# One of four heads' exponentials turned by VectorE and DMA instead of TensorE

## The chip, the core and the metric

The kernel runs on one core of a Trainium2 chip. A core has TensorE (PE in the profile; PEld is its weight load), VectorE (DVE), ScalarE (ACT), GpSimd (POOL) and SyncE (SP), which here does nothing but issue DMAs, and 16 DMA engines that move data between DRAM and the on-chip memory. The engines run their own queues in order and wait for each other through semaphores. The metric is the device time of one execution in microseconds (us), as the median of several runs.

## What is computed

A layer over 16 sequences of 128 positions with 512 channels, each with a context of 2048 rows. It has three parts: cross-attention with 16 heads of 32 channels, a selective state-space block (Mamba) with an MLP, and a mixture-of-experts output. The change touches the first part alone:

```python
q = queries @ wq.T + bq
k = context @ wk.T + bk
v = context @ wv.T + bv
...
attn = jnp.einsum('bhnd,bhsd->bhns', q, k) * scale
attn = jax.nn.softmax(attn, axis=-1)
out = jnp.einsum('bhns,bhsd->bhnd', attn, v)
```

Everything is float32.

## The kernel before

**Steps.** The attention is cut into 256 steps `u` (`NU`): 16 sequences, for each four blocks of 512 context rows (`sb`), for each four groups of four heads (`hg`). One step handles 128 queries x 512 context rows for four heads. The rest of the layer rides along in the same loop: the keys and values of the next block of context (`product`, L240, in a scheme that saves products), the input projections, the scans and the output projections of the state-space block (from step 54 on the scans run beside the attention), so that each step carries the attention of four heads and a piece of other work. After step 255 the MLP and the experts follow (`feed`).

**The order is written by hand.** The pool is under a manual schedule: each engine runs its instructions in the order in which the Python code emits them. The loop at the end of `perceiver_layer` emits, in each step: the loads of the step on SyncE (`load_bc`, `load_ctx`, the entries of `loads`); `scores(u)`; `weighted(u - 1)`; `maxima(u)`; the first products of the next context block (`x_products`); `exps(u)`; the first scan; `hold` and `x_sums`, which empty the two product banks; the four `turn(u, i)`, with other pieces of PE work (`late`) before the last one where a bank is needed; the second scan; `inner` work on VectorE; and `y_products`, the second part of the products.

**What a step of attention does.** `scores` (L302) fills four PSUM banks, one per head: 128 queries on partitions, 512 context rows along. `maxima` (L310) takes each row's maximum with VectorE. `exps` (L320) writes the exponentials of the four heads into one tile `pr` (128 queries x 4 heads x 512 rows; one buffer) with ScalarE and keeps the row sums. The weighted product needs the context rows on partitions, so `turn(u, i)` transposes, for the i-th 128 rows, the 128x128 blocks of the four heads with TensorE against an identity (L333) into a PSUM bank. ScalarE copies that bank to the tile `pT` (L338); in most steps VectorE makes the copy for `i == 2` (L336). `weighted(u)`, emitted in the next step behind that step's scores, multiplies the values `v` by the four `pT` tiles (L346), the four heads on four groups of 32 output partitions:

```python
for i in range(4):
    for j in range(4):
        nc.tensor.matmul(avp[j * HD : (j + 1) * HD, hg, :], vts[...][...],
                         pts[u, i][:, j, :], start=(i == 0), stop=(i == 3))
```

**SyncE's queue.** All loads of the loop and the few stores go through SyncE, in program order. An issue waits there until the buffer that it fills is free, and what is behind it waits too. The `c` tiles of the context (L154), the weight tiles `ws` (six buffers, shared by the attention's weights L167 and L169, `win` L504 and `wout` L509) and the broadcast rows `bc` (L601, two buffers each) are loaded a step or more before they are used. The rows `bcd` are the one thing that goes through DRAM and comes back at once: written at L593, read at L601.

Of the kernel before, what the change touches and what calls it, by code (L numbers as in the profile page):

```python
# [8 lines left out]
FP = mybir.dt.float32  # L9
# [6 lines left out]
P = 128  # L16
# [18 lines left out]
def perceiver_layer(ctx: ExitStack, tc: tile.TileContext, a: dict, out: bass.AP):  # L35
    nc = tc.nc

    const = ctx.enter_context(tc.tile_pool(name="const", bufs=1))
    dram = ctx.enter_context(tc.tile_pool(name="dram", bufs=1, space=DRAM))

    ident = const.tile([P, P], FP, tag="ident", name="ident")
# [14 lines left out]
    zd = [dram.tile([NQ, D], FP, tag=f"zd{b}", name=f"zd{b}") for b in range(B)]  # L56
    xnd = [dram.tile([NQ, D], FP, tag=f"xnd{b}", name=f"xnd{b}") for b in range(B)]
    bcd = [dram.tile([2 * DS, GT], FP, tag=f"bcd{g}", name=f"bcd{g}") for g in range(B // GB)]

    mv = const.tile([P, B, 2], FP, tag="mv", name="mv")  # L60
    rstd = const.tile([P, B], FP, tag="rstd", name="rstd")
# [47 lines left out]
    with ExitStack() as es:  # L109
# [5 lines left out]
        pool = att.enter_context(tc.tile_pool(name="att", bufs=2))  # L115
# [9 lines left out]
        banks = [psum.tile([P, 512], FP, tag=f"s{j}", name=f"bank{j}") for j in range(4)]  # L125
        avp = psum.tile([P, 4, P], FP, tag="av", name="avp")
        hst = psum.tile([P, NH // 2, GT], FP, tag="h0", name="hst")
        pa = psum.tile([P, 2, 256], FP, tag="pa", name="pa")
        pc = psum.tile([P, 2, 256], FP, tag="pc", name="pc")
# [5 lines left out]
        scale = float(HD) ** -0.5  # L135
        nc.vector.tensor_scalar_mul(bq, bq, scale)

        ctx_t, kts, vts, qts, prs, pts, avs, stats, xts = ({} for _ in range(9))
        wfac, cfac, held = {}, {}, {}

        def heads(ps):
            return ps.rearrange("p (k q) -> p k q", q=P)

        def halves(ps):
            return ps.rearrange("p (k q) -> p k q", q=256)
# [36 lines left out]
        def split(u):  # L182
            return u // 16, u // 4 % 4, u % 4
# [113 lines left out]
        def scores(u):  # L297

            b, sb, hg = split(u)
            for j in range(4):  # L300
                rows = slice(j * HD, (j + 1) * HD)
                nc.tensor.matmul(  # L302
                    banks[j], qts[b][rows, hg, :], kts[u // 4, hg][rows, :], start=True, stop=True
                )
            del kts[u // 4, hg]
# [8 lines left out]
        def exps(u):  # L314
            b, sb, hg = split(u)
            nm, sm = stats[b]
            pr = pool.tile([P, 4, 512], FP, tag="pr", name=f"pr{u}", bufs=1)
            for j in range(4):
                h = hg * 4 + j
                nc.scalar.activation(  # L320
                    pr[:, j, :],
                    banks[j],
                    AF.Exp,
                    bias=nm[j][:, sb, hg : hg + 1],
                    accum_out=sm[:, sb, h : h + 1],
                )
            prs[u] = pr

        def turn(u, i, bank):

            ps = heads(banks[bank])
            for j in range(4):
                nc.tensor.transpose(ps[:, j, :], prs[u][:, j, i * P : (i + 1) * P], ident)  # L333
            pT = pool.tile([P, 4, P], FP, tag="pT", name="pT", bufs=4)
            if i == 2 and u % 16 > 2:
                nc.vector.tensor_copy(pT, ps)  # L336
            else:
                nc.scalar.copy(pT, ps)  # L338
            pts[u, i] = pT

        def weighted(u):

            b, sb, hg = split(u)
            for i in range(4):
                for j in range(4):
                    nc.tensor.matmul(  # L346
                        avp[j * HD : (j + 1) * HD, hg, :],
                        vts[u // 4, hg // 2, i // 2][
                            :, i % 2, hg % 2 * P + j * HD : hg % 2 * P + (j + 1) * HD
                        ],  # L350
                        pts[u, i][:, j, :],
                        start=(i == 0),
                        stop=(i == 3),
                    )
            for i in range(4):
                del pts[u, i]
            del prs[u]
            if hg == 3:
                t = keep.tile([P, 4, P], FP, tag="avs", name=f"avs{b}_{sb}", bufs=4)
                nc.scalar.copy(t, avp)  # L360
                avs[b, sb] = t
# [825 lines left out]
        for g in range(NG):  # L1187
            p = 32 * (g + 1)
# [36 lines left out]
        put(inner, NU, lambda: give_back(flat(pa)))  # L1225


        ways = (("k", pa, pc, "u2"), ("v", halves(banks[0]), halves(banks[1]), "u2v"))

        def first_products(of, ph):  # L1230
            x_products(of, 0, ph, *dict((w[0], w[1:3]) for w in ways)[of])
# [44 lines left out]
        ps = banks[2]  # L1276
# [8 lines left out]
        for u in range(last):  # L1285
            live = u < NU
            g, r = divmod(u - 32 - LAG, 32)
            scans = 0 <= g < NG

            made, phase = divmod(u + 3, 4)  # L1290
            makes = 0 < made < B * SB
            of, phase = ("k", "v")[phase // 2], phase % 2
            load_bc(u + 2 - 32 - LAG, 0)
            if u % 4 == 1 and made + 1 < B * SB:
                load_ctx(made + 1, ("c00", "c10", "c11"))
            if u % 4 == 2 and made + 1 < B * SB:
                load_ctx(made + 1, ("c01",))
            for f in loads.get(u, ()):
                f()
            if scans and u <= NU:  # L1300
                decays(g, r, 0)
            if u > NU:
                while fed < feeds * (u - NU) // (last - 1 - NU):
                    feed(fed)
                    fed += 1
                if scans:
                    decays(g, r, 0)
            load_bc(u + 1 - 32 - LAG, DS)
            if u == NU + 1:
                load_rows()  # L1310
            if live:
                scores(u)
            if 1 <= u <= NU:
                weighted(u - 1)
            if u == NU:
                att.close()
                give_back(*banks, flat(avp))
                open_ffn()
            for f in early.get(u, ()):
                f()  # L1320
            if u == NU + 8:
                load_wex()
            for f in head.get(u, ()):
                f()
            if live:
                maxima(u)
            if makes:
                x_products(of, made, phase, pa, pc)
            if live:
                exps(u)  # L1330

            turns = ("t1", "t2", "t3", "t4") if u % 16 == 5 else ("t1", "t2")
            if makes and u % 4 == 1:
                ctx_sums(made, turns)
            for f in between.get(u, ()):
                f()
            if 0 <= u + 1 - 32 - LAG < 32 * NG:
                inputs(*divmod(u + 1 - 32 - LAG, 32))
            if makes and u % 4 == 1 and len(turns) == 2:
                ctx_sums(made, ("t3", "t4"))  # L1340
            silu_third()
            if scans:
                scan(g, r, 0)
            if makes:
                hold(of, made, pa, "u1")
            if scans:
                decays(g, r, 1)
            if makes:
                x_sums(of, made, phase, pa, pc)

            after_turns = late.get(u, ())
            places = [banks[(3 + i) % 4] for i in range(len(after_turns))]
            if live and after_turns:
                if u % 4 == 0:
                    places = [flat(avp), *places[:-1]]
                elif u % 2 and makes and u not in behind:
                    places[-1] = flat(pc)

            ahead = live and u % 16 in (3, 10) and len(after_turns) == 1
            if ahead:
                after_turns[0](banks[3])
                after_turns, places = (), ()
            taken = sum(any(p is b for b in banks) for p in places)
            if live:
                for i in range(3 if taken else 4):
                    turn(u, i, i)
            if scans:
                scan(g, r, 1)  # L1370
            for f in middle.get(u, ()):
                f()
            for f, ps in zip(after_turns, places):
                if live:
                    f(ps)
                else:
                    ps = bank()
                    f(ps)
                    give_back(ps)
            if live and taken:  # L1380
                turn(u, 3, (3 + taken) % 4)
            for f in behind.get(u, ()):
                ps = flat(pc) if makes else banks[2] if live else bank()
                f(ps)
                if not live:
                    give_back(ps)
            for f in after.get(u, ()):
                f()
            for f in inner.get(u, ()):
                f()  # L1390
            if makes:
                y_products(of, made, phase, pa, pc)
                y_sums(of, made, phase, pa, pc)
            silu_second()
# [76 lines left out]
```

## Time and profile before

| | |
|---|---|
| runs | 3761.74 us median of 3 (3761.29 to 3770.05) |
| span of the profiled execution | 3760.5 us |
| TensorE busy | 3722.9 us, 99% |
| VectorE busy | 2706.2 us, 72% |
| ScalarE busy | 2446.9 us, 65% |
| GpSimd busy | 2112.4 us, 56% |
| granted TensorE clock | 0.998 |
| transposes of the exponentials, L333 | 4096 instructions, 508.2 us |
| copies of them by ScalarE, L338 | 816, 434.4 us |
| copies of them by VectorE, L336 | 208, 143.9 us |
| weighted products, L346 | 8192 instructions, 276.7 us |
| DMA | 548.42 MB, mean 146 GB/s |

The profile is one execution, taken by the hardware profiler. An engine's busy time is the time in which at least one of its instructions ran. A group of instructions is given by its source line, engine and operation, `out<-in` by the program's tile names, the count, the busy time of the group, the mean ns of one and the idle time of the engine just before them with what ended it. A view called the timeline lists instructions in order of time, with their start, their duration and their count where neighbours are merged; the chain that ended last follows back from the last instruction through whatever released each step. SyncE's rows are DMA issues; "to landing" counts from the issue until the data are there.

### The profile page before, as it was taken

How to read it: one execution, taken by the hardware profiler on the slowest of the kernel's cores; microseconds unless marked ns; L12 is line 12 of the kernel's file. 1: busy time of each engine (PE TensorE's matmuls, PEld its weight loads, DVE VectorE, ACT ScalarE, POOL GpSimd, SP SyncE). 2: the span in 40 equal slices, each digit the busy share in tenths (PEclk: the TensorE clock that was granted, in tenths of full speed). 3: DMA queues.
4: the chain of work that ended last, by engine and by line, in shares of the span. 5: the costliest groups of instructions: out<-in, count | busy, mean ns of one | idle time of the engine just before them, and what ended most of it. 6: DMA issues, size and time to landing. Idle time of an engine off the chain costs nothing.

```text
span 3760.5 us, 70389 instructions
## 1 busy us (share of the span) xinstructions
PE 3722.9 (99%) x26120; PEld 2851.7 (76%) x26120; DVE 2706.2 (72%) x4854; ACT 2446.9 (65%) x5848; POOL 2112.4 (56%) x1969
## 2 busy tenths in 40 slices
PE   9999999999999999999999999999999999999999
PEld 7878787778777887888787878787778776655655
DVE  3444445887878777877788778877887877778843
ACT  4555556777767776777677767776777775545431
POOL 2111213676767666765666666766675667567820
PEclk9999999999999999999999999999999999999999
DMA  3111122344444535353534453445444448676752
GB/s 102 35 40 43 49 71 83 127 152 150 132 165 142 158 115 186 124 165 116 190 124 149 136 184 128 150 135 172 141 151 139 162 166 312 205 267 244 248 191 82
DMA packets 343225, 548.42 MB, mean 146 GB/s; under 512 B 24368, under 2 KB 227408, under 8 KB 342624
## 3 DMA queue, kind: packets, MB, share of 16 engines
q1 hardware_dynamic: 342432, 543.27, 43.5%
q8 instruction: 206, 3.38, 0.4%
q14 instruction: 139, 1.14, 0.1%
q0 software_dynamic: 448, 0.63, 0.1%
HBM read 527.29 MB, written 16.52 MB: 145 GB/s over the span
## 4 chain that ended last, share of the span: by engine, by line
PE 94%; DVE 2%; DMA 1%; ACT 1%; issue 1%; POOL 0%; SPq 0%; DVEq 0%; ACTq 0%; POOLq 0%
PE pa L240 24%; PE pc L240 17%; PE bank L333 12%; PE bank L302 7%; PE avp L346 7%; PE bank L531 5%; PE bank L942 4%; PE bank L911 2%; PE bank L1043 2%; PE bank L472 2%; PE avp L399 1%; PE bank L716 1%; PE pc L716 1%; PE avp L942 1%; PE pa L911 1%; PE pc L531 1%
## 5 line engine op out<-in xcount | busy, mean ns | idle before, releaser
L310 DVE TENSOR_REDUCE nm<-bank 128x1 f32<-128x512 f32 x1024 | 635.5, 683 | 225.2 <-PE bank L302 225.0
L703 POOL TENSOR_TENSOR ysum<-ysum,w 128x512 f32<-128x512 f32 x384 | 500.2, 1303 | 487.4 <-DVE hst L666 309.0
L320 ACT ACTIVATE pr<-bank,nm 128x512 f32<-128x512 f32 x1024 | 690.6, 688 | 90.9 <-DVE nm L310 85.3
L652 POOL TENSOR_TENSOR w<-dx,bc 128x512 f32<-128x512 f32 x512 | 655.9, 1302 | 8.9
L687 DVE TENSOR_TENSOR_SCAN hst<-hst,w 128x512 f32<-128x512 f32 x459 | 561.1, 1222 | 42.8 <-ACT hst L673 33.6
L338 ACT COPY pT<-bank 128x512 f32<-128x512 f32 x816 | 434.4, 586 | 177.2 <-PE bank L333 173.2
L673 ACT ACTIVATE hst<-dt,alog 128x254 f32<-128x254 f32 x918 | 439.4, 479 | 112.0 <-DVE hst L666 95.8
L333 PE MATMUL bank<-ident,pr 128*128 128x128 f32 x4096 | 508.2, 273 | 3.3 <-ACT pr L320 2.8
L333 PEld LDWEIGHTS bank<-ident,pr 128*128 128x128 f32 x4096 | 468.2, 141 | 47.1 <-issue 11.1
L346 PEld LDWEIGHTS avp<-pT,v 128*32 128x32 f32 x8192 | 208.0, 109 | 194.4 <-issue 176.6
L690 DVE TENSOR_TENSOR w<-hst,bc 128x512 f32<-128x512 f32 x459 | 317.4, 692 | 20.8 <-DMA bc<-bcd 5.2
L232 POOL TENSOR_TENSOR t<-c,c 128x512 f32<-128x512 f32 x128 | 163.1, 1274 | 257.6 <-PE pc L240 253.5
L302 PE MATMUL bank<-kt,qT 32*128 32x512 f32 x2048 | 296.0, 641 | 0.5 <-ACT pT L338 0.5
L346 PE MATMUL avp<-pT,v 128*32 128x128 f32 x8192 | 276.7, 276 | 0.0
L240 PE MATMUL pa<-t,ks 128*128 128x256 f32 x1024 | 248.6, 386 | 0.0
L240 PE MATMUL pa<-vs,t 128*128 128x256 f32 x1008 | 244.7, 386 | 0.0
L240 PEld LDWEIGHTS pa<-vs,t 128*128 128x128 f32 x1008 | 185.4, 190 | 34.6 <-issue 10.1
L240 PEld LDWEIGHTS pa<-t,ks 128*128 128x128 f32 x1024 | 184.8, 190 | 35.2 <-issue 11.6
L320 ACT ACTIVATION_READ_ACCUMULATOR pr<-bank,nm 128x1 f32 x1024 | 210.2, 205 | 0.0
L336 DVE COPY pT<-bank 128x512 f32<-128x512 f32 x208 | 143.9, 692 | 87.3 <-PE bank L333 85.6
L531 PE MATMUL bank<-zT,win 128*128 128x256 f32 x808 | 185.1, 379 | 0.0
L232 POOL TENSOR_TENSOR t<-c,t 128x512 f32<-128x512 f32 x128 | 163.7, 1279 | 36.1 <-issue 19.2
(320 smaller groups left out, 6889.0 us busy)
## 6 DMA issues: line engine op xcount, KB each, us to landing
bc<-bcd SPq DMA_DIRECT2D x512, 512.0 KB, 4.3
c<-in_ctxT_dram SPq DMA_DIRECT2D x256, 256.0 KB, 4.4
wf<-in_w_dram SPq DMA_DIRECT2D x124, 512.0 KB, 6.8
wqo<-in_wqkvo_dram SPq DMA_DIRECT2D x128, 256.0 KB, 4.8
win<-in_win_dram SPq DMA_DIRECT2D x128, 256.0 KB, 4.3
wout<-in_wout_dram SPq DMA_DIRECT2D x128, 256.0 KB, 4.2
x<-in_x_dram SPq DMA_DIRECT2D x16, 256.0 KB, 4.0
x1d<-x SPq DMA_DIRECT2D x16, 256.0 KB, 2.1
```

The source lines that it names most:

```text
L240: nc.tensor.matmul(ps[:, r, :], l[:, kc, r * P : (r + 1) * P], m[:, kc, :], start=(i in (1, 2, 5) and r == 0 and kc == 0), stop=(r == 1 an ...
L302: nc.tensor.matmul(banks[j], qts[b][rows, hg, :], kts[u // 4, hg][rows, :], start=True, stop=True)
L310: nc.vector.tensor_reduce(stats[b][0][j][:, sb, hg : hg + 1], banks[j], AX.X, ALU.max, negate=True)
L320: nc.scalar.activation(pr[:, j, :], banks[j], AF.Exp, bias=nm[j][:, sb, hg : hg + 1], accum_out=sm[:, sb, h : h + 1],)
L333: nc.tensor.transpose(ps[:, j, :], prs[u][:, j, i * P : (i + 1) * P], ident)
L338: nc.scalar.copy(pT, ps)
L346: nc.tensor.matmul(avp[j * HD : (j + 1) * HD, hg, :], vts[u // 4, hg // 2, i // 2][:, i % 2, hg % 2 * P + j * HD : hg % 2 * P + (j + 1) * HD],
L531: nc.tensor.matmul(ps, w[:, kc, :], zTs[g][:, kc, :], start=(kc == 0), stop=(kc == KC - 1))
L652: nc.gpsimd.tensor_tensor(w, dx.unsqueeze(1).to_broadcast([P, NH // 2, GT]), bcs[g * 32 + r, 0][:, i * NH // 2 : (i + 1) * NH // 2, :], AL ...
L673: nc.scalar.activation(bt(h[:, k, :])[:, :, 1:], bt(dt)[:, :, 1:], AF.Exp, scale=aneg[:, ec, n : n + 1],)
L687: nc.vector.tensor_tensor_scan(flat, flat, w.rearrange("p n t -> p (n t)"), 0.0, ALU.mult, ALU.add)
L703: nc.gpsimd.tensor_tensor(s, s, w, ALU.add)
```

## The change

Head 0 of each step's four heads no longer goes through TensorE and PSUM to get its context rows onto partitions. A new function `blocks(u)`, emitted right behind `exps(u)`, does it: VectorE transposes head 0's exponentials (128 queries x 512 rows) in blocks of 32x32 within each group of 32 partitions into the tile `tr`, SyncE writes that tile to DRAM (`trd`, 256 KB, two places in turn), and four further DMAs of 64 KB, one for each group of 32 partitions, read it back so that context row `c * 32 + k` of each 128 lies on partition `c * 32 + k`, in the tile `pd`. `turn` transposes the other three heads alone, and ScalarE now makes all four copies, of 128x384 in place of 128x512; VectorE's copy for `i == 2` is gone. `weighted` reads head 0 from `pd`, at 32 neighbouring columns at a time, and the others from `pT`. A tile of the start-up takes the tag `tr` in place of one of its own, so that the two share a buffer.

```diff
+    trd = [dram.tile([P, 512], FP, tag=f"trd{i}", name=f"trd{i}") for i in range(2)]
...
+        def blocks(u):
+
+            t = pool.tile([P, 4, 4, 32], FP, tag="tr", name=f"tr{u}", bufs=1)
+            nc.vector.transpose(
+                t.rearrange("p c i q -> p i c q"),
+                prs[u][:, 0, :].rearrange("p (i c k) -> p i c k", i=4, c=4),
+            )
+            d = trd[u % 2]
+            nc.sync.dma_start(d, t.rearrange("p c i q -> p (c i q)"))
+            pd = pool.tile([P, 4, 4, 32], FP, tag="pd", name=f"pd{u}", bufs=1)
+            for c in range(4):
+                nc.sync.dma_start(
+                    pd[c * 32 : (c + 1) * 32].rearrange("k a i q -> k a (i q)"),
+                    d.rearrange("(a k) (c r) -> c k a r", k=32, c=4)[c],
+                )
+            pds[u] = pd
+
         def turn(u, i, bank):
 
-            ps = heads(banks[bank])
-            for j in range(4):
-                nc.tensor.transpose(ps[:, j, :], prs[u][:, j, i * P : (i + 1) * P], ident)
-            pT = pool.tile([P, 4, P], FP, tag="pT", name="pT", bufs=4)
-            if i == 2 and u % 16 > 2:
-                nc.vector.tensor_copy(pT, ps)
-            else:
-                nc.scalar.copy(pT, ps)
+            ps = heads(banks[bank])[:, 1:4, :]
+            for j in range(3):
+                nc.tensor.transpose(ps[:, j, :], prs[u][:, j + 1, i * P : (i + 1) * P], ident)
+            pT = pool.tile([P, 3, P], FP, tag="pT", name="pT", bufs=4)
+            nc.scalar.copy(pT, ps)
             pts[u, i] = pT
...
-                        pts[u, i][:, j, :],
+                        pts[u, i][:, j - 1, :] if j else pds[u][:, :, i, :],
...
-        ways = (("k", pa, pc, "u2"), ("v", halves(banks[0]), halves(banks[1]), "u2v"))
+        ways = (("k", pa, pc, "u2"), ("v", halves(banks[0]), halves(banks[1]), "tr"))
...
             if live:
                 exps(u)
+                blocks(u)
```

More of the change, by code (lines that the diff above doesn't have):

```diff
@@ L136, in perceiver_layer @@
         nc.vector.tensor_scalar_mul(bq, bq, scale)
-        ctx_t, kts, vts, qts, prs, pts, avs, stats, xts = ({} for _ in range(9))
+        ctx_t, kts, vts, qts, prs, pts, avs, stats, xts, pds = ({} for _ in range(10))
         wfac, cfac, held = {}, {}, {}
@@ L356, in weighted @@
                 del pts[u, i]
-            del prs[u]
+            del prs[u], pds[u]
             if hg == 3:
```

## The prediction

> **What bounds the kernel now.** I read the busy shares first, then the chain that ended last, then TensorE's timeline step by step, then SyncE's.
>
> ```profile
> PE 3722.9 (99%) x26120; PEld 2851.7 (76%) x26120; DVE 2706.2 (72%) x4854; ACT 2446.9 (65%) x5848; POOL 2112.4 (56%) x1969
> ...
> PE 94%; DVE 2%; DMA 1%; ACT 1%; issue 1%; POOL 0%; SPq 0%; DVEq 0%; ACTq 0%; POOLq 0%
> ...
> L333 PE MATMUL bank<-ident,pr 128*128 128x128 f32 x4096 | 508.2, 273 | 3.3 <-ACT pr L320 2.8
> ```
>
> TensorE is busy 99% and holds 94% of the chain: whatever it no longer does comes off the end, as long as nothing else makes it wait. The transposes (L333) are 4096 instructions; the 273 ns of one overlap with their neighbours', so I take their spacing from the timeline. This is a short step, 49, from its scores (L302) to the next step's; engine by engine:
>
> ```profile
> 583.92 1.14 PE L302 MATMUL bank<-kt,qT 32*128 32x512 f32 x8
> 584.99 1.08 PE L346 MATMUL avp<-pT,v 128*32 128x128 f32 x32
> ...
> 589.56 1.91 PE L333 MATMUL bank<-ident,pr 128*128 128x128 f32 x16
> 591.31 1.89 PE L240 MATMUL pa<-t,ks 128*128 128x256 f32 x8
> 593.13 1.14 PE L302 MATMUL bank<-kt,qT 32*128 32x512 f32 x8
> 594.20 1.07 PE L346 MATMUL avp<-pT,v 128*32 128x128 f32 x30
> ```
> ```profile
> 585.08 2.48 DVE L310 TENSOR_REDUCE nm<-bank 128x1 f32<-128x512 f32 x4 [1.75 <-PE bank L302]
> ```
> ```profile
> 585.81 0.69 ACT L320 ACTIVATE pr<-bank,nm 128x512 f32<-128x512 f32 x1 [1.19 <-DVE nm L310]
> ```
>
> To see here: TensorE has no hole, and the weighted product of step 49 (L346) comes in the next step, behind its scores: at 594.20, 10.28 us after step 49's scores began. That distance is the room which the new route has.
>
> **The gain.** The 16 transposes take 591.31 - 589.56 = 1.75 us, 0.109 us each. Four fewer in each of 256 steps is 256 x 0.437 = **112 us**. The weighted product keeps its 32 instructions.
>
> **The new route, per step.** VectorE reaches the transposition behind the four maxima: 585.08 + 2.48 - 583.92 = 3.64 us after the scores began (head 0's exponentials are out at 586.50, before that). Then:
> - one VectorE transposition of 128x512. No row shows one. Below, the 0.43 us of a 128x256 VectorE operation (L574; less than a pass over half the elements nothing suggests); above, the 1.22 us of the scan over 128x512 (L687). I take 0.70, the 692 ns of the 128x512 copy (L336), the nearest row: same size, one pass.
> - a 256 KB write to DRAM by SyncE. The nearest rows are the stores of the same size:
>
> ```profile
> c<-in_ctxT_dram SPq DMA_DIRECT2D x256, 256.0 KB, 4.4
> ...
> x1d<-x SPq DMA_DIRECT2D x16, 256.0 KB, 2.1
> ...
> zd<-xn SPq DMA_DIRECT2D x14, 256.0 KB, 2.0
> ...
> dtw<-in_dtproj_dram SPq DMA_DIRECT2D x64, 16.0 KB, 4.0
> ```
>
> The last column is the median from issue to landing: 2.0 for a store on its own.
> - four reads of 64 KB that wait for it. SyncE issues two loads of c in 0.88 us at 582.30, so the fourth starts about 1.25 after the first. The landing of a read is 4.0 to 4.4 at the median, but these medians hold the queue of other loads before them; the least for dtw and for c is 2.7 each, for 16 and for 256 KB alike. At this point of a step SyncE has issued nothing for some microseconds (it waited for VectorE), so I take 2.7; 4.3 stays as the upper end.
> - 0.1 for three wake-ups (an estimate: the bc load at 605.66 follows the landing of bcd, 604.18 + 1.5, at once).
>
> Sum: 3.64 + 0.70 + 2.0 + 1.25 + 2.7 + 0.1 = **10.4 us** after the scores began. TensorE now comes to the weighted product 0.44 earlier, at 9.84 in this step: it waits 0.55 us. Steps counted on TensorE's timeline, from scores to scores: 53 of 255 last about 9.2 us (wait 0.55), 22 about 9.6 (wait 0.1), 13 about 10.1 and 167 more (115 of them over 12) none. Cost: 53 x 0.55 + 22 x 0.1 = **32 us**. What is queued behind the waiting product is TensorE's whole step, but not the next step's exponentials: scores go ahead of the product, so their maxima run during the wait, and one wait doesn't lengthen the next route.
>
> **SyncE's order.** The write stands behind all loads of its step in one queue. In most steps these are issued before 4.3 us. In two steps of each 32 they wait for weight buffers that TensorE frees late. Step 139 begins at 1656.82:
>
> ```profile
> 1665.69 2.27 SPq L504 DMA_DIRECT2D win<-in_win_dram  x2
> 1668.05 1.04 SPq L601 DMA_DIRECT2D bc<-bcd  x2
> ```
>
> The write can go at about 1668.6, and 2.0 + 1.25 + 2.7 + 0.1 later, at 1674.6, the tile is there. TensorE comes at 1670.98 - 0.44 (its weighted product there): 4.1 us late, in steps 43, 75, 107 and so on, 7 times. Step 150 is like it (bc at 1809.03, product at 1812.99): 2.9 us, 6 times. Together **46 us**. The other way round, loads of the next step now stand behind the route and start at about 8.5 us into a step. Most are wanted a whole step later and take 4.3, so I cost this at nothing; without that cover it is some 2 us for the two late wout loads of 16 steps, 32 us.
>
> **Edges.** Step 0 lasts 6.8 us and waits about 3, the last ones about 2: **5 us**.
>
> **VectorE and ScalarE.** VectorE loses 208 copies of 0.69 (L336) and gains 256 transpositions of 0.70, but the new ones stand in front of the first scan and the sum of the products that frees the bank of L240. That sum ended at 6.8 in step 150 and would end at 7.2, where TensorE can now come at 6.95 in even steps without other work: some 25 steps by 0.25, **6 us**. ScalarE makes all four copies, 128x384 now: between 0.42 (256 wide) and 0.53 (512 wide), 4 x 0.47 against 3.2 x 0.53 a step, nothing: its copies have the last product group as cover, 1.8 us in the shortest step. The shared start-up tile changes one write before step 0: nothing. In the scan stage the DMA engines are 46% busy instead of 22%; I add 0.1 us to the route of the short steps there, 60 x 0.13 = **8 us**.
>
> **Sum.** -112 + 32 + 46 + 5 + 6 + 8 = -15 on an execution of 3760.5 us span. The runs' median is 3761.74, 1.2 above the span; the same 1.2 stays around it. Forecast: **3746 us**.
>
> **A rule against the change.** The row: a transpose costs TensorE 0.109 us here, as one 128x128 float32 block. The Trainium skill, "VectorE: DVE Perf Modes", section "The three transpose paths" and the rules after it, gives 390 ns for TensorE and 311 ns for VectorE on 128x128 bf16, says that VectorE turns only 32x32 blocks, and sends a 128x128 transpose to TensorE. By its figure four blocks on VectorE would be 1.24 us, an estimate, 0.55 above my 0.70, and the sum would end near +20. Its 390 ns for TensorE doesn't fit the trace, so I stay with the copy's row.
>
> **Rivals.**
> 1. *The route is longer than the steps (slower).* Place: the wait of the weighted product in the 88 steps up to 10.1 us, then the 10.9 ones. Price: at a route of 11.35 the waits, stepped through all step lengths (a wait in one step gives the next step's route more room), sum to 115 us, and with 46 + 11 the kernel stands at +60: **3822**. It decides from about 10.7 on, only 0.3 above my sum. Any one of three does it: the transposition at the scan's 1.22 us (route 10.9, 3782), the reads nearer to their median (4.3: route 12.0, +116, 3878), or the transposition waiting for all four heads' exponentials, which end 1.0 us later, at 588.59 (route 11.4). For it: the margin is small and medians are what loaded queues give. Against: the queue is quiet at that moment, and the transposition reads head 0 alone.
> 2. *The route is hidden.* At 9.8 (transposition 0.55, last 64 KB read 2.3, being small) the short steps wait some 4 us in all: -112 + 4 + 46 + 11 = -51, **3711**. For it: the least landing of 2.7 also holds the traffic of a 256 KB load. Against: nothing shows a smaller read on its own.
> 3. *Nothing arrives.* TensorE's 0.44 us are given back to ScalarE's fourth copy or to VectorE's later sum instead: within 0.3%, **3760**. Against: TensorE has waited for neither (0.3 us in total for pT).
>
> **Chances.** Forecast 0.36 (0.25 of it faster by over 0.3%, 0.11 within; 0.3%, 11 us, is about what a measurement of this kernel can tell from no change), rival 1 0.38, rival 2 0.19, rival 3 0.07. Faster 0.44, same 0.18, slower 0.38. The bounds of the route alone (9.6 to 12.4) give 3700 to 3910; I keep 8 in 10 in 3680 to 3870, the forecast's own part being 3725 to 3765.
>
> **What would show it.** In the profile after: L333 x3072 with 0.33 us for three; TensorE's idle time before L346 ended by the DMA of the new tile, near 0.5 us in the 9.2 us steps and 3 to 4 us in steps 43, 75, 86, 107 and their like; the write's issue about 4.5 us after the scores; its landing 2.0 after; the last read's 2.7. Wrong would be: waits in the steps over 11 us outside those thirteen (the route is over 11.5), or none in the short ones (under 9.9), or a VectorE transposition far from 0.7.

## The result, and the profile after

The median went from 3762.43 us to **3906.68 us** (3900.2 to 3912.86), a ratio of 1.038 with an interval of 1.0365 to 1.0395: 144 us slower, where 15 us faster was forecast. The profiled execution took 3912.86 us, its span 3910.9 us, and the mean granted clock of TensorE fell from 0.998 to 0.977.

From the page of the kernel after (busy shares, chain by engine, three groups with "busy, mean ns of one | idle before, releaser", two kinds of DMA issue with the median us to landing):

```profile
PE 3695.0 (94%) x25096; PEld 2788.4 (71%) x25096; DVE 2713.1 (69%) x4902; ACT 2438.8 (62%) x6056; POOL 2116.4 (54%) x1969
...
PE 71%; DMA 11%; DVE 9%; ACT 3%; SPq 3%; issue 2%; POOL 1%; DVEq 0%; ACTq 0%; POOLq 0%
...
L361 PE MATMUL avp<-pd,v 128*32 128x128 f32 x2048 | 288.8, 287 | 146.6 <-DMA pd<-trd 143.9
L351 PE MATMUL bank<-ident,pr 128*128 128x128 f32 x3072 | 402.2, 274 | 15.3 <-DVE xnT L406 5.9
...
L333 DVE STREAM_TRANSPOSE tr<-pr 128x512 f32<-128x512 f32 x256 | 179.6, 701 | 48.0 <-ACT pr L321 47.9
...
trd<-tr SPq DMA_DIRECT2D x256, 256.0 KB, 2.1
pd<-trd SPq DMA_DIRECT2D x1024, 64.0 KB, 1.9
```

The transposes went as planned, 4096 to 3072 and 508.2 to 402.2 us busy. But TensorE's share fell from 99% to 94%, and its part of the chain from 94% to 71%: 11% of the span now runs through DMAs, 8 of them (5 and 3 in the chain by line) the two halves of the route, and 144 us of TensorE's idle time before the weighted product (L361) were ended by the tile that comes back from DRAM.

**A quiet step is as predicted.** Step 49 after, on TensorE, VectorE and SyncE (start, duration, engine, line):

```profile
578.12 1.14 PE L303 MATMUL bank<-kt,qT 32*128 32x512 f32 x8
...
583.76 1.47 PE L351 MATMUL bank<-ident,pr 128*128 128x128 f32 x12
...
587.97 0.30 PE L361 MATMUL avp<-pd,v 128*32 128x128 f32 x1
```
```profile
579.28 2.48 DVE L311 TENSOR_REDUCE nm<-bank 128x1 f32<-128x512 f32 x4 [1.76 <-PE bank L303]
581.68 0.70 DVE L333 STREAM_TRANSPOSE tr<-pr 128x512 f32<-128x512 f32 x1
```
```profile
582.41 0.34 SPq L338 DMA_DIRECT2D trd<-tr  x1
584.56 1.75 SPq L341 DMA_DIRECT2D pd<-trd  x4
```

The transposition starts 3.56 us after the scores and takes 0.70; the write is issued at 4.29, and its landing lets SyncE issue the reads at 6.44; they are there at 9.72, and the product begins at 9.85, with no hole on TensorE.

**A loaded step is not.** Steps 150 and 151 on SyncE, then the weighted product of step 150 on TensorE:

```profile
1855.31 8.65 SPq L524 DMA_DIRECT2D wout<-in_wout_dram  x6
1864.01 0.42 SPq L629 DMA_DIRECT2D dtw<-in_dtproj_dram  x1
1864.53 0.37 SPq L616 DMA_DIRECT2D bc<-bcd  x1
1864.99 0.38 SPq L338 DMA_DIRECT2D trd<-tr  x1
1870.59 1.75 SPq L341 DMA_DIRECT2D pd<-trd  x4
```
```profile
1867.32 1.14 PE L303 MATMUL bank<-kt,qT 32*128 32x512 f32 x8
1873.96 0.39 PE L361 MATMUL avp<-pd,v 128*32 128x128 f32 x1 [5.51 <-DMA pd<-trd]
...
1874.15 0.42 PE L361 MATMUL avp<-pd,v 128*32 128x128 f32 x1
...
1875.83 2.62 PE L241 MATMUL pa<-va,c 128*128 128x256 f32 x8
```

The write waits behind the loads of its step, as predicted, and then needs 5.6 us to land (1864.99 to 1870.59) and not 2.0. TensorE waits 5.51 us. What follows is slower as well: the first two pd products start 0.19 us apart (0.13 in step 49), and the group of L241 takes 2.62 us in place of 1.99. The same stretch in windows (busy us of PE, PEld, DVE, ACT and POOL, then the granted clock, the DMA engines' share and GB/s):

```profile
1850.40:1867.30 16.90, 14.18 (x93) 10.02 (x92) 11.40 (x22) 9.23 (x23) 15.44 (x15) 1.00 0.51 162
1867.30:1873.50 6.20, 1.16 (x9) 0.31 (x8) 4.92 (x7) 4.78 (x13) 0.72 (x1) 0.74 0.46 168
1873.50:1880.80 7.30, 6.83 (x56) 5.89 (x57) 0.58 (x2) 1.70 (x4) 1.27 (x1) 0.75 0.88 244
1880.80:1887.50 6.70, 6.70 (x20) 3.06 (x19) 2.07 (x4) 1.29 (x5) 1.27 (x1) 1.00 0.36 117
```

The clock is 1.00 before the wait, 0.74 and 0.75 in the wait and the 7.3 us behind it, 1.00 after: it was one half for 6.8 us. In the whole trace TensorE stood at half clock for 182.6 us in 35 pieces (before: 19.0 in 6), and its idle times over 0.1 us add up to 211 us (before: 32). That makes a sum to compare: +179 idle, at most +82 for the half clock (half of 164), -112 for the transposes: +149 if the half clock is lost in full, against 150 between the two profiled executions and 144 between the medians.

Four rows of the waits (total, times, longest) hold the rest of the story:

```profile
PE avp L361 <- DMA pd<-trd: 143.9, 68, 6.4
...
ACT avs L375 <- PE avp L361: 92.9, 64, 7.7
...
DVE tr L333 <- ACT pr L321: 47.9, 13, 7.1
```
```profile
SPq L341 <- DMA trd<-tr: 747.7, 256, 8.6
```

The last one is SyncE's: for 748 us it stands before the reads, for its own write to land, and can issue nothing else.

ScalarE waited 47.9 us for its copy of the weighted sums (L375, every fourth step) before and waits 92.9 now. That copy stands ahead of the next step's exponentials, so a late tile makes the next transposition late too: in step 140 it began 10.0 us after the scores.

### The profile page after: what moved, and what is told of

Same layout as the page of the kernel before. It is cut to its first block, busy times and chain, and to the rows that moved or that the text cites. A ratio compares the mean times of both kernels' runs of the same rounds, so it can differ in the third digit from the quotient of the medians.

```text
span 3910.9 us, 70932 instructions
## 1 busy us (share of the span) xinstructions
PE 3695.0 (94%) x25096; PEld 2788.4 (71%) x25096; DVE 2713.1 (69%) x4902; ACT 2438.8 (62%) x6056; POOL 2116.4 (54%) x1969
## 4 chain that ended last, share of the span: by engine, by line
PE 71%; DMA 11%; DVE 9%; ACT 3%; SPq 3%; issue 2%; POOL 1%; DVEq 0%; ACTq 0%; POOLq 0%
PE pa L241 18%; PE pc L241 14%; PE bank L351 6%; PE avp L361 6%; DMA trd<-tr 5%; PE bank L303 5%; PE bank L957 4%; PE bank L546 4%; DMA pd<-trd 3%; DVE nm L311 3%; PE bank L926 2%; PE bank L1058 2%; SPq L341 2%; DVE hst L702 2%; PE bank L487 1%
## 5 line engine op out<-in xcount | busy, mean ns | idle before, releaser
L353 ACT COPY pT<-bank 128x384 f32<-128x384 f32 x1024 | 423.5, 483 | 159.8 <-PE bank L351 157.8
L361 PEld LDWEIGHTS avp<-pd,v 128*32 128x32 f32 x2048 | 212.7, 114 | 343.9 <-issue 236.6
L361 PE MATMUL avp<-pd,v 128*32 128x128 f32 x2048 | 288.8, 287 | 146.6 <-DMA pd<-trd 143.9
L351 PE MATMUL bank<-ident,pr 128*128 128x128 f32 x3072 | 402.2, 274 | 15.3 <-DVE xnT L406 5.9
L351 PEld LDWEIGHTS bank<-ident,pr 128*128 128x128 f32 x3072 | 356.5, 141 | 64.6 <-issue 11.1
L361 PE MATMUL avp<-pT,v 128*32 128x128 f32 x6144 | 294.5, 288 | 0.0
L241 PE MATMUL pa<-t,ks 128*128 128x256 f32 x1024 | 260.0, 399 | 0.0
L241 PE MATMUL pa<-vs,t 128*128 128x256 f32 x1008 | 251.2, 393 | 0.0
L241 PEld LDWEIGHTS pa<-t,ks 128*128 128x128 f32 x1024 | 192.6, 198 | 39.6 <-issue 10.8
L361 PEld LDWEIGHTS avp<-pT,v 128*32 128x32 f32 x6144 | 218.1, 114 | 0.0
L241 PEld LDWEIGHTS pa<-vs,t 128*128 128x128 f32 x1008 | 190.2, 195 | 37.6 <-issue 11.2
L333 DVE STREAM_TRANSPOSE tr<-pr 128x512 f32<-128x512 f32 x256 | 179.6, 701 | 48.0 <-ACT pr L321 47.9
```

Source lines behind the costliest of these rows:

```text
L241: nc.tensor.matmul(ps[:, r, :], l[:, kc, r * P : (r + 1) * P], m[:, kc, :], start=(i in (1, 2, 5) and r == 0 and kc == 0), stop=(r == 1 an ...
L351: nc.tensor.transpose(ps[:, j, :], prs[u][:, j + 1, i * P : (i + 1) * P], ident)
L361: nc.tensor.matmul(avp[j * HD : (j + 1) * HD, hg, :], vts[u // 4, hg // 2, i // 2][:, i % 2, hg % 2 * P + j * HD : hg % 2 * P + (j + 1) * HD],
```

## The experiments

Two theories at first. **A, order:** the time is what TensorE waits for the route, because the route is late where SyncE's one queue has loads ahead of it; take the wait away and the gain is there. **B, traffic:** the 512 KB more of each step (548 to 683 MB in all) slow the other transfers everywhere.

### Nobody waits for the route

```diff
-                        pts[u, i][:, j - 1, :] if j else pds[u][:, :, i, :],
+                        pts[u, i][:, max(j - 1, 0), :],
```

> The route runs in full (transposition, write, four reads in every step) but the weighted product of head 0 reads head 1's transposed tile instead of the route's, so that TensorE waits for nothing of it; the output is wrong for head 0 of each group. Theory A (order): all of the loss is TensorE's waits for the route, because the write stands behind loads in SyncE's queue and its data behind theirs in the DMA engines, plus the half clock that follows long waits. Without the wait the 112 us of the transposes come off: 3650 to 3675 us, granted clock back at 0.995 or more. Theory B (traffic): the 512 KB more per step and the five more issues delay loads and other engines whoever waits for the route: still above 3760 us.

Measured: **3802.21** (3796.73 to 3806.36), ratio 1.011 (1.0094 to 1.0127). A kernel whose TensorE never waits for the route is still some 40 us slower than before: A falls in this form. Step 151 on TensorE and on SyncE, and TensorE's two largest waits:

```profile
1810.31 5.32 PE L731 MATMUL bank<-wout,zs 128*128 128x512 f32 x12
1822.86 3.44 PE L731 MATMUL bank<-wout,zs 128*128 128x512 f32 x4 [7.23 <-DMA wout<-in_wout_dram]
```
```profile
1810.82 0.42 SPq L616 DMA_DIRECT2D bc<-bcd  x1
1811.34 0.38 SPq L338 DMA_DIRECT2D trd<-tr  x1
1818.24 1.74 SPq L341 DMA_DIRECT2D pd<-trd  x4
1820.09 0.85 SPq L524 DMA_DIRECT2D wout<-in_wout_dram  x2
```
```profile
PE bank L731 <- DMA wout<-in_wout_dram: 43.9, 6, 8.1
PE pc L731 <- DMA wout<-in_wout_dram: 24.3, 6, 5.1
```

SyncE issued its last load at 1810.82 and the write at 1811.34; it then stood for 6.9 us until the write had landed, issued the four reads, and came to the wout loads at 1820.09. TensorE had wanted these since 1815.6. In the kernel before, the scores of this step start at 1811.92; TensorE and SyncE there:

```profile
1818.87 7.03 PE L716 MATMUL bank<-wout,zs 128*128 128x512 f32 x16
```
```profile
1819.92 1.19 SPq L509 DMA_DIRECT2D wout<-in_wout_dram  x2
```

In the kernel before the loads go out 1.05 us after the first product of this group, and the 16 products run without a hole; with the route in front of them it is 9.78 us.

These two are not loads of the next step, and not all of `wout` is loaded a step ahead. There are six buffers for eight tiles; the preceding step loads six, and the last two are issued by the output projection itself (L739), as its first products set buffers free, in the step that multiplies with them. So in SyncE's order they stand behind the route of their own step. Such a place comes twice in 32 steps (steps 23 and 25 of each 32), twelve times in all, at 5.7 us each, and the clock falls to one half as well (90 us in 15 pieces in the whole trace).

### The step's loads behind the route

```diff
+            def step_loads():
+                load_bc(u + 2 - 32 - LAG, 0)
+                ...
                 exps(u)
                 blocks(u)
+                step_loads()
+                load_bc(u + 1 - 32 - LAG, DS)
```

> The same kernel as the changed one, but each step's loads are issued by SyncE behind the route's write and reads instead of in front of them. Theory A: the write goes at 4.3 us after the scores in nearly every step and lands 2 us later, the route ends near 9.7, the waits over 2 us vanish and with them the half clock: 3665 to 3720 us. Theory B: the same traffic, so 3850 us or more.

Measured: **3977.22**, ratio 1.0572 (1.0556 to 1.0587), slower than the change itself. The waits of TensorE:

```profile
PE bank L351 <- ACT pT L353: 43.8, 17, 3.7
PE avp L361 <- DVE v L271: 35.5, 15, 3.4
PE pc L241 <- DVE kt L261: 31.6, 12, 3.6
PE bank L731 <- DMA wout<-in_wout_dram: 29.7, 6, 6.3
...
PE avp L361 <- DMA pd<-trd: 9.0, 12, 2.3
```
```profile
DVE w L705 <- DMA bc<-bcd: 165.3, 63, 7.2
```

The wait for the tile falls from 144 to 9 us, as A has it, but the loads are now late (VectorE waits 165.3 us for the rows `bc`, 5.2 before), and the engines that use them make TensorE wait longer than before. The queue is short of room in both orders: whichever goes first makes the other late.

### The route in every second step

```diff
-                blocks(u)
+                if u % 2 == 0:
+                    blocks(u)
```

In the odd steps all four heads go the old way; the four `pT` tiles of a step become one whose first quarter the route fills.

> The route in even steps alone, which last 10.9 us or more; odd steps use TensorE for all four heads as before. Loads stay in front of the write. Theory A: half the gain, 56 us, and only the held even steps (22 of each 32, and what is left of 12) keep long waits, some 6 x 5 us: 3725 to 3750 us. Theory B, loss in proportion to the traffic: half of the 144 us, near 3830 us.

Measured: **3807.69**, ratio 1.0124 (1.0109 to 1.014), nearer to B's number than to A's. But by steps the loss isn't spread. Step 23 of each 32 grew by 8.2 us and step 25 by 3.7, while step 12, whose tile comes from an odd step and so the old way, became 0.44 shorter.

### The route in ScalarE's queue

```diff
-            nc.sync.dma_start(d, t.rearrange("p c i q -> p (c i q)"))
+            nc.scalar.dma_start(d, t.rearrange("p c i q -> p (c i q)"))
...
                     turn(u, i, i)
+                    if i == 1:
+                        come_back(u)
```

The four reads go out of `come_back`, by ScalarE too.

> The route's write is issued from ScalarE's queue behind the exponentials, its reads from there behind the second of the four copies of the turns. Theory A: SyncE's queue no longer holds the route; the reads go out some 7.3 us after the scores and land at 10.5 to 11, so short steps wait about 1 us and no step waits over 3: 3700 to 3770 us, clock 0.99 or more. Theory B: 3850 us or more.

Measured: **4175.7** in a single run. The waits of TensorE:

```profile
PE bank L303 <- ACT pT L357: 152.0, 57, 8.7
PE avp L365 <- DMA pd<-trd: 64.1, 36, 3.6
```

SyncE no longer stands still, but ScalarE does. One step on its queue:

```profile
1999.77 0.34 ACTq L338 DMA_DIRECT2D trd<-tr  x1
...
2006.23 1.76 ACTq L345 DMA_DIRECT2D pd<-trd  x4
```

In 97 of the 256 steps the reads go out within 0.2 us of the write's landing, so that ScalarE stood for it, and issuing the four takes 1.76 us of its time here and 1.4 or more in every step. Its copies of `pT` queue behind, and TensorE waits for the bank that they empty. The write itself lands no sooner. Where five or more of SyncE's transfers were in flight, ScalarE's write took 6.6 us at the median (15 cases), SyncE's own 6.0 (45 cases, kernel after). The Trainium skill, "DMA: Bandwidth & Descriptors", section "Issuing engines are not separate DMA queues", says the same: DMAs of different engines run on the same 16 DMA engines.

So a second pair of theories. **A2, places:** route and loads block each other at a few steps, 22 and 24 of each 32 above all. **B2, spread:** every route costs something.

### Every second step, two of 32 spared

```diff
-                if u % 2 == 0:
+                if u % 2 == 0 and u % 32 not in (22, 24):
```

> The route in even steps alone, and not in steps 22 and 24 of each 32. Theory A2 (places): the loss sits where the route and the loads block each other in SyncE's one queue: a write behind loads that wait for weight buffers (step 22, paid in 23), and wout loads that step 25 wants at once behind the route of step 24. The even run paid 8.2 us in each step 23 and 3.7 in each step 25, six times, 71 us; without these two routes 3807 - 71 = 3736: 3725 to 3750 us, faster than before. Theory B2 (spread): the DMA traffic of the route and its issues slow loads everywhere, and steps 23 and 25 are only where it shows; other steps then take the wait over, 3765 us or more.

Measured: **3739.75** (3737.33 to 3741.4), ratio 0.9937 (0.9922 to 0.9952): 68 us less than with these 16 routes, and faster than before. From its page:

```profile
PE 3680.9 (99%) x25672; PEld 2803.5 (75%) x25672; DVE 2714.4 (73%) x4886; ACT 2435.2 (65%) x5928; POOL 2113.5 (57%) x1969
...
PE 90%; DVE 5%; DMA 2%; ACT 2%; issue 1%; POOL 0%; SPq 0%; DVEq 0%; ACTq 0%; POOLq 0%
```

TensorE is back at 99%, with half clock for 15 us.

### All steps but seven of 32

```diff
-                if u % 2 == 0:
+                if u % 32 not in (5, 11, 21, 22, 23, 24, 25):
```

> The route in all steps except 5, 11 and 21 to 25 of each 32. Theory A2: the five places of long waits (steps 6, 12, 22, 23 and 25, 167 us in the changed kernel) return to their old length, and what is left is the gain of 200 steps less what VectorE's later work costs in short steps (steps 0, 2, 18, 26 were 0.2 to 1.3 us longer): 3700 to 3735 us, granted clock back above 0.99. Theory B2: 3770 us or more.

Measured: **3754.27** (3747.29 to 3762.72), ratio 0.9978 (0.9968 to 0.9988): between the ranges of the two theories. TensorE still waits 36.4 us for the tile, 40 times, 2.0 us at most. The seven spared steps have their old length again, as A2 has it. The others are together 26 us longer than with VectorE's transposition alone (next section), and 23 of these sit in steps 10, 13, 14 and 28 of each 32, where TensorE waits for the tile of the step before. So the list of places was too short. What the route costs in many steps is VectorE's transposition, as the next runs show.

### VectorE's transposition alone, and neither

The first keeps the transposition and drops the DMAs; the second drops both. In both head 0 reads head 1's tile.

```diff
-            d = trd[u % 2]
-            nc.sync.dma_start(d, t.rearrange("p c i q -> p (c i q)"))
...
-            pds[u] = pd
```

> VectorE transposes head 0 in every step, but no DMA follows and head 0's product reads head 1's tile; the output is wrong for head 0 of each group. It gives the cost of the transposition's place in VectorE's order by itself: the gain of 112 us less 6 by the prediction (3656 us), less some 45 by the steps that were longer without any wait in the run with the unused route (3695 us): 3685 to 3705 us by theory A2. If traffic made those steps longer (B2), 3650 to 3665.

> Neither transposition nor DMA: head 0 isn't turned at all and its product reads head 1's tile; the output is wrong for head 0 of each group. It gives what the smaller work of TensorE and the four copies on ScalarE are worth by themselves: by both theories 112 us less, 3645 to 3660 us. If ScalarE's fourth copy takes part of it back, above 3670.

Measured: **3703.93**, ratio 0.9843 (0.9828 to 0.9858), and **3663.41**, ratio 0.9735 (0.9721 to 0.975). Three heads alone save 99 us and not 112, and the transposition costs 40.5. Where: step 130 with the transposition alone, whose scores start at 1518.41, on VectorE and on TensorE:

```profile
1519.05 0.95 DVE L446 TENSOR_TENSOR sm<-sm,nm 128x64 f32<-128x64 f32 x1
...
1521.15 2.47 DVE L311 TENSOR_REDUCE nm<-bank 128x1 f32<-128x512 f32 x4
1523.55 0.69 DVE L333 STREAM_TRANSPOSE tr<-pr 128x512 f32<-128x512 f32 x1
...
1526.20 0.88 DVE L261 SCALAR_TENSOR_TENSOR kt<-pc,bk,u1k 128x256 f32<-128x256 f32 x2
```
```profile
1527.13 1.99 PE L241 MATMUL pc<-c,ks 128*128 128x256 f32 x8 [1.11 <-DVE kt L261]
```

Before, the maxima of this step began 2.07 us after its scores and the sum of the products (kt) 6.52 after; here it is 2.74 and 7.79. VectorE was at work up to the end of step 129. With that step's transposition it comes to the maxima 0.24 us later than before, counted from the scores of step 129, while TensorE comes to the scores 0.43 earlier; the transposition of step 130 itself adds 0.6. TensorE wants the bank that kt frees and waits 1.11.

The first of the two runs also decides on theory B, since it differs from "nobody waits" in the DMAs of the route alone. Step by step, from scores to scores, the two traces differ by 90 us in sum: the twelve steps 23 and 25 are 91 us longer with the DMAs, and the other 243 steps together 1 us shorter. So as long as nobody waits for the route, its 512 KB per step cost nothing outside the places where a load is wanted at once.

### The chosen steps, and the two bad places alone

```diff
-                if u % 2 == 0:
+                if u % 16 not in (5, 9) if u < 40 else u % 32 in (2, 4, 6, 8, 10, 12, 14, 15, 16, 18, 20, 28, 30):
```
```diff
-                if u % 2 == 0:
+                if u >= 54 and u % 32 in (22, 24):
```

> The route only where the runs so far show room for it: in the first 40 steps all but 5 and 9 of each 16, after that steps 2, 4, 6, 8, 10, 12, 14, 15, 16, 18, 20, 28 and 30 of each 32. Theory A2 (places): from the run with the spared even steps (22 us faster), 5 more for steps 0 and 26, which grew by 0.4 six times each, and 3 and 8 for step 15 and the odd early steps: 3720 to 3735 us. Theory B2 (spread): more routes, more loss, 3740 us or more.

> The route in steps 22 and 24 of each 32 alone, 12 steps in all, from step 54 on; the other 244 use TensorE for all four heads. Theory A2: the two places cost by themselves what they cost in the even run, 6 x (8.2 + 3.7) less 12 x 0.44: 66 us, 3815 to 3840 us, with the granted clock at one half for some microseconds after each wait. Theory B2: 12 of 256 routes carry little traffic: 3760 to 3775 us.

Measured: **3736.32** (3729.97 to 3737.95), ratio 0.9922 (0.9909 to 0.9936), the fastest of the kernels that do the whole work and 1 us above the range of A2, and **3821.24** (3816.39 to 3824.23), ratio 1.0151 (1.0137 to 1.0165). The second is the sharpest of the tests: 14 routes in 256 steps (the expectation counted 12), 7 MB more, and 58 us slower. Step 23 of each 32 grew by 7.7 us and step 25 by 3.1. A2 holds for the large part.

## Why the prediction was wrong

Taken apart by subtraction of runs, against the terms of the sum:

| part | runs | predicted | measured |
|---|---|---|---|
| three heads on TensorE | before to neither | -112 | -99 |
| VectorE's transposition in its place | to transposition alone | 6 | 40 |
| the route's DMAs in SyncE's queue, nobody waits | to nobody waits | 0 (32 without cover) | 98 |
| TensorE waits for the route | to after | 32 + 46 + 5 + 8 = 91 | 104 |
| sum | | -15 | +144 |

**The step that failed** is this one: "loads of the next step now stand behind the route and start at about 8.5 us into a step. Most are wanted a whole step later and take 4.3, so I cost this at nothing". It was 98 us. The cover was named rightly as the two late wout loads, but priced at 2 us a step. They are not loads of the next step: they belong to the step whose route they stand behind, which needs them at once. They wait for the full time in which SyncE is held, from the write's issue to the last read's: 8.6 us in the step shown above (1811.34 to 1819.98). And ten of the twelve waits bring half clock with them (not those of 3.20 and 3.68 us). Between the traces of "transposition alone" and "nobody waits", TensorE's idle time grew by 68 us (63 to 131) and its half clock by 68 us (22 to 90), of which at most half is lost: 102 at most, against 91 between these two executions and 98 between the medians.

**The write's landing** was the second miss, and it lies under the first. "2.0 for a store on its own" holds for a write on its own. Worked out from the trace after, by the number of loads still in flight when the write was issued:

```
loads in flight    writes    issue to landing, median us
0                  112       1.98
1                   30       2.00
2                   18       3.38
3                   25       3.00
4                   26       5.48
5 or more           45       5.96
```

The Trainium skill, "DMA: Bandwidth & Descriptors", section "Queues, rings and completion order", has descriptors of one ring taken up in ring order; the rows here agree with a write that starts behind the loads issued just before it. The prediction counted the wait for SyncE to *issue* those loads, and not the wait for them to *move*. So the products of steps 11 and 22 of each 32 (43, 75 and 86, 118 among them) wait 5.4 to 6.4 us in most groups (predicted 4.1 and 2.9; 71 us against 46). Those of steps 5, 21 and 24, whose write was issued in time (4.3 us after the scores in steps 133, 149 and 165, 5.4 in step 152), still wait for 49 us together; in these four the write lands 4.3 to 6.0 us after its issue.

**"One wait doesn't lengthen the next route"** is wrong in every fourth step, where ScalarE's copy of the weighted sums stands ahead of the exponentials (92.9 against 47.9 us). The price of this alone wasn't measured.

**The short steps** wait almost nowhere: the route there took 9.72 us after the scores and not 10.4, because the last read of 64 KB lands in 1.9 us or so and not in 2.7. Of the 32 us forecast for them (53 x 0.55 + 22 x 0.1 is 31) some 10 came, outside the products of steps 5 and 21. "None in the short ones (under 9.9)" was named as a sign that the working was wrong, and it was one. The other sign came too: steps over 11 us outside the thirteen waited some 26 us, most of it for the tiles of steps 24, 9 and 13 of each 32. That 91 forecast for TensorE's waits stand near 104 measured is partly luck: some 22 too much here, 74 too little in the five products above. The waits themselves are 144 us; the runs' difference is smaller, although the half clock grows from 90 to 183 us, because a TensorE that is late anyway waits less for wout (71 us where nobody waits for the route, 9 after).

**VectorE's place**, 6 forecast and 40 measured, was the third miss. The working looked at the sum of the products in one step (150) and took 0.25 us in 25 steps. It left out that VectorE may still be busy from the step before, so that two transpositions count. By steps of 32, 0, 2, 18, 26 and 8 lose 0.5 to 0.9 us each, and 3, 4, 19 and 20 some 0.3 to 0.4.

**Right** were the transposition (0.70 us; 0.701 measured), the count and price of TensorE's transposes within 12 us, the landing of a lone write, and the two places where SyncE's own loads hold the route. **Rival 1**, "the route is longer than the steps", named the right sign, but its 3822 came from another mechanism, the short steps; the route is short there, and long where the queue is full. The time lies above the range, whose 3870 had no term for the loads behind the route.

Open in part is where the 12 us between -112 and -99 went. In most steps the full 0.44 us came off; 10 of the missing 12 sit in steps 2, 3, 19 and 26 of each 32. In step 98, with three heads alone, TensorE is early and waits 0.51 us for VectorE's sum of the products; ScalarE made all four copies of that step before, too, so its fourth copy isn't the cause there. The other steps were not taken apart. Nor was a kernel tried whose wout loads are issued a step earlier, which would take more buffers.

## What to carry to other kernels

A DMA that waits for another DMA's landing holds its whole queue for that time: look at what stands behind it in the tightest steps, loads that the same step issues later among them, and ask when each is wanted, not at the average step. Price such a wait by the landing that the queue gives at that point, with the transfers already in flight ahead of it, and add the clock that TensorE loses in a wait of some microseconds. Where a change has bad places, put it only in the others: the same route that costs 144 us everywhere gains some 27 in chosen steps.

## What the runs showed of the hardware

- **Half clock comes in pieces.** In the trace after, 34 of 35 pieces last 3.41 or 6.83 us. Behind the span's start, all 21 idle times of TensorE from 2.8 us up have such a piece, and 11 of the 16 from 1.9 to 2.8. The piece starts 1.2 to 5.1 us after the wait began. It is no fixed rule: where nobody waits for the route, idle times of 2.86, 3.20 and 3.68 us had none. The Trainium skill, "TensorE: Matmul & The Clock Gate", section "HAM oscillation — how this bites in real kernels", gives as a rule that idle gaps stay under some 3.4 us; the length of the pieces agrees with the window of that page, but gaps of 1.9 to 2.74 us had one here too.
- **A 64 KB read back from DRAM** lands in 1.9 us at the median, four of them 3.3 us after the first is issued.
- **VectorE's transposition** of 128x512 float32 in 32x32 blocks takes 701 ns, about as long as its copy of the same size before (692 ns).
